# Three dense tiles of a graph-attention layer: turned matmuls, masked in place in SBUF

## The chip, the cores and the metric

The kernel runs on one core of one Trainium2 chip. The metric is the device time of one execution in microseconds (us). The time before is the median of three runs. One more execution was taken with the hardware profiler.

## The reference

Four graph-attention layers follow each other on 3327 nodes with 512 features. All use one sparse 0/1 adjacency matrix. Each layer normalizes its input, cuts it at zero, attends over the neighbours and adds the result to its input. The last layer, which the change touches, has eight heads of 64 features:

```python
Wh = jnp.einsum('ni,hio->hno', h, W)
f1 = jnp.einsum('hno,ho->hn', Wh, a1)
f2 = jnp.einsum('hno,ho->hn', Wh, a2)
e = jax.nn.leaky_relu(f1[:, :, None] + f2[:, None, :], ALPHA)
masked = jnp.where(adj[None] > 0, e, NEG_INF)
attention = jax.nn.softmax(masked, axis=-1)
h_prime = jnp.einsum('hnm,hmo->hno', attention, Wh)
```

The exponential of a leaky relu of a sum is a product of two exponentials, or a second product of two, whichever is larger. So the weight of a pair is, up to factors that cancel or go into the features, `max(a*b - 1, 0) + 1`. Here `a` belongs to the target node, `b` to the source node, and a factor `c` of the source is put on its features.

## The kernel before

**Tiles.** The nodes are padded to 3328, which is 26 tiles of 128 targets. They were ranked by degree before, so that tile 0 holds the nodes with most neighbours. `CAPS` says how many neighbours a tile's nodes may have: 36 for tile 0, 22 for tile 3, 11 for tile 25.

**List tiles.** In the last layer the tiles 25 down to 3 work from lists of neighbours. A step takes four columns of the list. `fetch` issues one indirect DMA (a gather, L835, on POOL) for each column but the first. Each brings 128 rows of 528 numbers from a table in DRAM into a buffer g. The first column is the node itself and comes by an ordinary DMA. There are five g buffers, and fetches run five steps ahead (`LOOK`). `scored` makes the weights: DVE adds (L888) and takes the leaky relu (L890), ACT takes the exponential into PSUM (pw, L891). `group` multiplies rows by weights on DVE (L919, 512 numbers a column, into a buffer m) and adds the columns up on PE with an identity as the stationary operand (L924, 512 columns into a PSUM bank). `divisors` and `means` (L942) divide, `added` (L958) adds the input, and `scatter` (L843) sends the tile out by an indirect DMA on POOL. All in all there are 360 gathers, 26 scatters and 105 steps.

**Dense tiles.** The tiles 0 to 2 (`DENSE[3] = 3`) attend to all 26 source blocks, with a mask of bytes for the adjacency. Class `Several` does this in two passes of four heads. The two passes over 26 blocks give 52 units `u`. For each unit:

- `load` brings the block's features (v, three buffers) and its mask (mk, three buffers), two DMAs on SP (L1259, L1260).
- `weights` makes four relus of 384 targets on ACT (L1276) into PSUM tile r, of which there is one.
- `features` scales the block's features by c on ACT (L1287) and puts c behind them (L1288), 65 numbers a head, into vs (two buffers).
- `masked` adds 1 and multiplies by the mask on DVE (L1292), one instruction over 1536 numbers, from r into e (two buffers in SBUF).
- `products` runs 12 matmuls on PE (L1310), one for each head and tile. The weights of 128 targets are stationary and the features of one head move. They are 65 columns, which `twice` doubles to 130. The results lie side by side in two PSUM banks, which a matmul with zeros (L1302) clears at the start of a pass.

At the end of a pass `means` (L1328, L1329) divides by the 65th column.

**The order.** PE, DVE, ACT and POOL execute their instructions in the order that is written. `later(s, place, piece)` hangs a piece of dense work on step `s`, ahead of `scored` ("first"), after it ("scored") or after `group` ("last"). `place` spreads the 52 units over the steps:

```python
for u in range(2 * NT):
    s = s0 + u * (s1 - s0) // (2 * NT)
    later(s, "first", lambda u=u: self.masked(u))
    later(s, "scored", lambda u=u: (self.weights(u + 1), self.features(u + 1), self.load(u + 3)))
    later(s + 1, "first", lambda u=u: self.products(u))
```

Here s0 is 0 and s1 is the number of steps less 8, so a unit comes about every 1.9 steps.

The other layers have no part in the change. Layer 1 uses `Several` for one tile of four heads, layer 2 has nine dense tiles of its own kind.

Of the kernel before, what the change touches and what calls it, by code (L numbers as in the profile page):

```python
# [18 lines left out]
P = 128  # L19
# [777 lines left out]
def tile_gat_lists(ctx: ExitStack, tc: tile.TileContext, x, adj, ws, avs, out, ident, half, slots, L, low, spare, tabx, tabs):  # L797
# [417 lines left out]
    class Several:  # L1215
# [3 lines left out]
        def __init__(self, l, n, W):  # L1219
            self.l, self.n, self.H, self.D = l, n, HEADS[l], F // HEADS[l]  # L1220
            self.Q = Q = self.H // 2
            self.DV = DV = self.D + 1
            self.tiles = [Tile(l, t, W) for t in range(n)]
            room = Room(low, L, spare, *([pools["e"].tile([P, 8 * BANK], F32, name="room", bufs=1)] if n > 1 else []))
            self.a = room(self.H * n * P).rearrange("p (h c) -> p h c", h=self.H)

            y = self.a.rearrange("p h c -> p (h c)")[:, -n * F:]
            self.y = [y[:, q * F:(q + 1) * F] for q in range(n)]
            self.e = [room(Q * n * P).rearrange("p (h c) -> p h c", h=Q) for _ in range(2)]
            self.c, self.b = [room(NT * Q * 2).rearrange("p (j h) -> p j h", j=NT) for _ in range(2)]  # L1230

            self.vs = [room((Q + (self.H == 8)) * DV) for _ in range(2)]
# [6 lines left out]
            self.per = BANK // DV - (self.H == 8)  # L1239

        def begin(self):

            if self.H == 8:
                for vs in self.vs:
                    nc.scalar.activation(vs[:, self.Q * self.DV:], ident[:, :self.DV], AF.Copy, scale=0.0)
# [49 lines left out]
        def products(self, u):  # L1295

            Q, DV = self.Q, self.DV
            j, e, vs = u % NT, self.e[u % 2], self.vs[u % 2]
            if j == 0:
                self.po = [pools["w"].tile([P, BANK], F32, name="whole") for _ in range(0, self.n * Q, self.per)]  # L1300
                for o in self.po:
                    nc.tensor.matmul(o, ident, zero.to_broadcast([P, BANK]), start=True, stop=False,  # L1302
                                     skip_group_check=True)
            for q in range(self.n):
                for h in range(Q):
                    o, o0 = self.where(q, h)
                    dst, mov = o[:, o0:o0 + DV], vs[:, h * DV:(h + 1) * DV]
                    if self.H == 8:
                        dst, mov = twice(dst, self.per * DV - o0), twice(mov, (Q - h) * DV)
                    nc.tensor.matmul(dst, e[:, h, q * P:(q + 1) * P], mov, start=False, stop=(j == NT - 1),  # L1310
                                     skip_group_check=True)

        def where(self, q, h):
            i = q * self.Q + h
# [18 lines left out]
        def place(self, s0, s1):  # L1333
# [12 lines left out]
            for q in range(self.n):  # L1346
                self.tiles[q].ends(s + 1 + 2 * q)

    at = {}

    def later(s, place, piece):
        at.setdefault((s, place), []).append(piece)
# [8 lines left out]
    for l in range(NL):  # L1361
        W, following = following, None
        if l == NL - 1:
            before.close()
        with ExitStack() as c2:
            def pool(name, bufs, **kw):
                return c2.enter_context(tc.tile_pool(name=f"{name}{l}", bufs=bufs, **kw))

            turning, projecting = [], []
            psum = dict(space=bass.MemoryType.PSUM)  # L1370
            whole = HEADS[l] == 1
            pools = {"o": pool("ps_o", 1 if whole else 2, **psum)}
            if l < NL - 1:
                pools.update(t=pool("ps_t", 1, **psum))
            if whole:
                pools.update(w=pool("ps_w", 3, **psum), e=pool("epool", 1))
                wholes = Wholes(l, W)
                pw = L[:, :BANK]
            else:
                pools.update(m=pool("mpool", 5))  # L1380
                pools.update(p=pool("ps_p", 1 if DENSE[l] else 2, **psum))
                if DENSE[l]:
                    pools.update(w=pool("ps_w", l // 3 + 1, **psum), r=pool("ps_r", 1, **psum))
                    if DENSE[l] > 1:
                        pools.update(e=pool("epool", 1))
                    wholes = Several(l, DENSE[l], W)
                    pw = pools["p"].tile([P, BANK], F32, name="pw")
            if not whole:

                for _ in range(2):  # L1390
                    nc.tensor.matmul(pools["o"].tile([P, BANK], F32, name="bank"), ident,
                                     zero.to_broadcast([P, BANK]), start=True, stop=True)
            if DENSE[l]:

                scores = itertools.cycle([pw[:, :BANK // 2], pw[:, BANK // 2:]])
            else:
# [84 lines left out]
```

## Time and profile before

| | |
|---|---|
| median of 3 runs | 2442.68 us (2439.82 to 2448.11) |
| profiled execution | 2959.5 us, span 2957.8 us |
| mean granted clock of PE | 0.867 |
| first gather of the last layer | 2296 us |
| PE, DVE, ACT, POOL busy in the last layer (662 us) | 524, 410, 204, 367 us |
| L924, 512 columns | 720 instructions in the layer's program, 0.43 us from start to start |
| L1310, 130 columns | 1248 instructions, 24 in 2.68 us |
| L1292, 1536 numbers | 52 instructions, 1.75 us each |
| L1276, 384 numbers | 208 instructions, 0.58 us each |
| L835, a gather | 0.95 us busy, 1.25 us from start to start |

The profiled execution is 517 us longer than the median, so its stretches are not stretches of a plain run. In the profile a matmul of 32-bit numbers is two instructions, each with a weight load of its own (PEld). A group's line shows its count, busy time, the mean of one, and the idle time of its engine just before, with what ended it. "issue" is waiting for which the profile shows nothing; "remote" is a wait whose end it can't put down to an instruction. A busy share says little here: POOL's next gather starts 0.30 us after the last one's busy time ends.

### The profile page before, as it was taken

Reading aid. Unit: us, or ns where it says so; the run is one execution under the profiler, and the core shown is the slowest. Engines: PE = TensorE matmul, PEld = TensorE weight load, DVE = VectorE, ACT = ScalarE, POOL = GpSimd, SP = SyncE. Lnnn points to the kernel's source line nnn. Section 1 sums busy time; section 2 is a strip of 40 time slices with the busy share of each in tenths; the row PEclk is TensorE's granted clock in tenths of the full one; section 3 lists DMA queues with packets and bytes.
Section 4 is the critical chain, followed back from the end, with each engine's and each line's share of the span. In section 5 each row is a group of like instructions: output and inputs, shape, how many; then the busy total and the mean of one; then the engine's idle time right before and its main releaser. Section 6 shows DMA issues by size and latency. Waiting matters only on the chain.

```text
span 2957.8 us, 27080 instructions
## 1 busy us (share of the span) xinstructions
PE 2224.7 (75%) x7082; PEld 1251.4 (42%) x7082; DVE 1914.3 (65%) x4968; ACT 931.8 (32%) x2502; POOL 1728.5 (58%) x1717
## 2 busy tenths in 40 slices
PE   4777677787677745788877787689696778877887
PEld 2664243343333323344434344245354445444453
DVE  7887656565546523767765565698887556666665
ACT  5882122222221101323332222344333333333330
POOL 7894465565556663555655552676764555555554
PEclk9988788888888877899988889799897889988898
DMA  6885477677666675666766663788775666666664
GB/s 229 322 294 160 140 218 216 193 235 222 188 205 195 189 194 170 181 202 192 209 193 189 192 192 111 226 264 257 236 248 152 191 177 184 185 182 194 185 187 137
DMA packets 260730, 594.20 MB, mean 201 GB/s; under 512 B 103699, under 2 KB 121107, under 8 KB 256214
## 3 DMA queue, kind: packets, MB, share of 16 engines
q0 software_dynamic: 124368, 432.13, 49.8%
q1 hardware_dynamic: 132454, 153.45, 16.5%
q10 hardware_dynamic: 3744, 6.82, 0.7%
q8 instruction: 57, 0.93, 0.1%
q14 instruction: 107, 0.88, 0.1%
HBM read 542.60 MB, written 49.65 MB: 200 GB/s over the span
## 4 chain that ended last, share of the span: by engine, by line
DVE 21%; PE 18%; issue 16%; another core or an unknown queue 11%; ACT 6%; POOL 4%; DMA 3%; DVEq 0%; ACTq 0%; POOLq 0%; SPq 0%
PE bank L924 11%; DVE m L919 9%; POOL g L835 3%; PE pv L469 3%; PE whole L1310 3%; DVE bank L912 2%; DMA g<-tab,idxb 1%; DVE z L890 1%; DVE z L888 1%; ACT r L1276 1%; DVE x L962 1%; DVE q L439 1%; ACT pw L891 1%; DVE room L1292 1%
## 5 line engine op out<-in xcount | busy, mean ns | idle before, releaser
L924 PE MATMUL bank<-m,ident 128*128 128x512 f32 x2414 | 1236.5, 659 | 268.9 <-DVE m L919 137.5
L835 POOL DMA_INDIRECT g<-tab,idxb x712 | 678.2, 952 | 465.5 <-issue 189.3
L919 DVE TENSOR_TENSOR m<-g,pw 128x512 f32<-128x512 f32 x1207 | 752.0, 682 | 267.6 <-ACT pw L891 193.5
L924 PEld LDWEIGHTS bank<-m,ident 128*128 128x128 f32 x2414 | 490.2, 211 | 879.8 <-issue 568.9
L469 PE MATMUL pv<-w,hT 128*128 128x264 f32 x1664 | 447.4, 423 | 107.0 <-ACT hT L458 71.2
L835 POOL DMA_INDIRECT g<-tabx,twiceb x342 | 324.1, 948 | 245.8 <-issue 124.4
L835 POOL DMA_INDIRECT g<-tab,idxa x297 | 283.1, 953 | 262.1 <-DMA tab<-v 88.5
L469 PEld LDWEIGHTS pv<-w,hT 128*128 128x128 f32 x1664 | 339.5, 208 | 215.2 <-ACT hT L458 79.6
L891 ACT ACTIVATE pw<-z 128x32 f32<-128x32 f32 (+4 forms) x356 | 67.8, 190 | 945.4 <-DVE z L890 509.8
L1162 PE MATMUL whole<-ve,em 128*128 128x512 f32 x468 | 224.5, 632 | 48.2 <-DVE em L1135 27.9
L1310 PE MATMUL whole<-L,room 128*128 128x130 f32 x1248 | 171.1, 288 | 79.2 <-issue 79.0
L1310 PEld LDWEIGHTS whole<-L,room 128*128 128x128 f32 x1248 | 163.1, 201 | 107.1 <-issue 104.7
L695 POOL TENSOR_TENSOR key<-a,keys 128x3328 int32<-128x3328 int32 (+1 forms) x29 | 189.5, 6539 | 15.9 <-DVE cand L704 12.6
L912 DVE SCALAR_TENSOR_TENSOR bank<-g,L,bank 128x512 f32<-128x512 f32 x243 | 183.3, 754 | 9.9 <-remote 2.0
L835 POOL DMA_INDIRECT g<-tabx,twicea x99 | 94.4, 954 | 119.6 <-issue 75.3
L1162 PEld LDWEIGHTS whole<-ve,em 128*128 128x128 f32 x468 | 92.8, 203 | 158.7 <-issue 114.6
L451 PE MATMUL pt<-ident,xn 128*128 128x128 f32 x416 | 74.5, 302 | 93.0 <-issue 32.2
L704 DVE MAX8 cand<-key 128x8 f32<-128x208 int32 x416 | 143.6, 363 | 0.1
L890 DVE SCALAR_TENSOR_TENSOR z<-z 128x32 f32<-128x32 f32 (+5 forms) x428 | 82.5, 193 | 91.4 <-remote 61.4
L919 DVE TENSOR_TENSOR bank<-g,pw 128x512 f32<-128x512 f32 x74 | 51.5, 696 | 126.7 <-ACT pw L891 105.6
L1276 ACT ACTIVATE r<-low,L 128x384 f32<-128x384 f32 x208 | 121.2, 582 | 9.8 <-remote 3.9
L888 DVE TENSOR_TENSOR z<-g,pw 128x32 f32<-128x32 f32 (+4 forms) x356 | 61.8, 174 | 94.9 <-DMA g<-tab,idxa 39.0
(181 smaller groups left out, 2154.4 us busy)
## 6 DMA issues: line engine op xcount, KB each, us to landing
a<-in_adj SPq DMA_DIRECT2D x25, 1664.0 KB
tab<-v SPq DMA_DIRECT2D x78, 264.0 KB
ve<-tab SPq DMA_DIRECT2D x78, 264.0 KB
g<-tab SPq DMA_DIRECT2D x65, 264.0 KB
tabx<-vx SPq DMA_DIRECT2D x26, 528.0 KB
g<-tab,idxb POOLq DMA_INDIRECT x712
low<-tab SPq DMA_DIRECT2D x52, 132.0 KB
spare<-tab SPq DMA_DIRECT2D x52, 132.0 KB
```

Of the source, the lines that this page charges most:

```text
L469: nc.tensor.matmul(pv[:, s, :HF + 8], hT[:, k, :], W.w[:, k, s, :], start=(k == 0), stop=(k == KC - 1))
L695: nc.gpsimd.tensor_tensor(key[:, c:c + quarter], a[:, c:c + quarter], keys[:, c:c + quarter], OP.mult)
L704: nc.vector.max(cand[:, g * 8:(g + 1) * 8], key[:, g * SEG:(g + 1) * SEG])
L835: nc.gpsimd.indirect_dma_start(out=out_, out_offset=None, in_=table, in_offset=bass.IndirectOffsetOnAxis(ap=which, axis=0))
L890: nc.vector.scalar_tensor_tensor(z, z, SLOPE, z, OP.mult, OP.max)
L891: nc.scalar.activation(self.wt[:, k0:k0 + n, :H], z, AF.Exp)
L912: nc.vector.scalar_tensor_tensor(acc, v, w, acc, OP.mult, OP.add)
L919: nc.vector.tensor_tensor(out_.rearrange("p (s h d) -> p s h d", s=2, d=D), v.rearrange("p s (h d) -> p s h d", d=D), wt[:, k0 + q, :H].re ...
L924: nc.tensor.matmul(self.po, ident, m[:, q, :], start=False, stop=(k0 + q == K - 1), skip_group_check=True)
L1162: nc.tensor.matmul(tl.po.rearrange("p (s m) -> p s m", s=2), e[:, q * P:(q + 1) * P], v.rearrange("p (s m) -> p s m", s=2)[:, :, :F // 2], ...
L1276: nc.scalar.activation(self.r[:, h, :], self.a[:, g, :], AF.Relu, bias=-1.0, scale=self.b[:, j, g:g + 1])
L1310: nc.tensor.matmul(dst, e[:, h, q * P:(q + 1) * P], mov, start=False, stop=(j == NT - 1), skip_group_check=True)
```

## The change

The last layer's dense tiles get a class of their own, `Turned`; `Several` is left to layer 1 and loses what only eight heads needed. In `Turned` the operands of the matmul change places. The scaled features of one head (65 columns) are stationary, and the weights of all three tiles (384 columns) move. So a unit has 4 matmuls in place of 12, and the results of a head (65 x 384) take one PSUM bank, four banks for a pass. The relus are written to the SBUF buffer e, and the mask is applied there in place. The buffers e, vs, v and mk are rings of four. At the end of a pass ACT copies the sums to SBUF, PE turns them back, 65 x 128 at a time, and DVE divides. The units are spread in half steps, and there are four steps between the passes.

```diff
+    class Turned:
+        def __init__(self, l, n, W):
+            self.l, self.n, self.H, self.Q, self.D = l, n, HEADS[l], 4, F // HEADS[l]
+            self.DV = self.D + 1
+            self.passes = self.H // self.Q
...
+            self.e = [room(self.Q * wide).rearrange("p (h c) -> p h c", h=self.Q) for _ in range(4)]
+            self.sums = self.a[:, self.Q:, :]
...
+            self.vs = [room(self.Q * self.DV) for _ in range(4)]
+            self.v = [room(self.Q * self.D + 8) for _ in range(4)]
+            self.mk = [room(n * P // 4).bitcast(U8) for _ in range(4)]
...
+        def weights(self, u):
...
+            e = self.e[u % 4]
+            for h in range(Q):
+                nc.scalar.activation(e[:, h, :], self.a[:, h0 + h, :], AF.Relu, bias=-1.0,
+                                     scale=self.b[:, j, h0 + h:h0 + h + 1])
+
+        def features(self, u):
...
+            vs = self.vs[u % 4].rearrange("p (h d) -> p h d", d=self.DV)
+            for h in range(Q):
+                nc.scalar.activation(vs[:, h, :D], self.v[u % 4][:, h * D:(h + 1) * D], AF.Copy,
+                                     scale=self.c[:, j, h0 + h:h0 + h + 1])
+            nc.scalar.activation(vs[:, :, D], self.c[:, j, h0:h0 + Q], AF.Copy)
+
+        def masked(self, u):
+            n = self.n * P
+            nc.vector.scalar_tensor_tensor(self.e[u % 4], self.e[u % 4], 1.0,
+                                           self.mk[u % 4].unsqueeze(1).to_broadcast([P, self.Q, n]), OP.add, OP.mult)
+
+        def products(self, u):
+            j, e, vs, DV = u % NT, self.e[u % 4], self.vs[u % 4], self.DV
+            if j == 0:
+                self.po = [pools["w"].tile([P, BANK], F32, name="whole") for _ in range(self.Q)]
+            for h, o in enumerate(self.po):
+                nc.tensor.matmul(o[:DV, :self.n * P], vs[:, h * DV:(h + 1) * DV], e[:, h, :], start=(j == 0),
+                                 stop=(j == NT - 1))
+
+        def summed(self):
+            for h, o in enumerate(self.po):
+                nc.scalar.activation(self.sums[:self.DV, h, :], o[:self.DV, :self.n * P], AF.Copy)
+
+        def turned(self, q):
+            DV = self.DV
+            self.pt = pools["x"].tile([P, BANK], F32, name="turned")[:, :self.Q * DV].rearrange("p (h d) -> p h d", d=DV)
+            for h in range(self.Q):
+                nc.tensor.transpose(self.pt[:, h, :], self.sums[:DV, h, q * P:(q + 1) * P], ident[:DV, :DV])
...
+        def place(self, s0, s1):
+            later(s0 - 1, "first", self.begin)
+            for u in range(4):
+                later(s0 - 1, "first", lambda u=u: self.load(u))
+            later(s0 - 1, "scored", lambda: (self.weights(0), self.features(0)))
+            halves = 2 * (s1 - s0 - 4 * (self.passes - 1))
+            for u in range(self.passes * NT):
+                i, j = divmod(u, NT)
+                s, b = divmod(2 * (s0 + 4 * i) + u * halves // (self.passes * NT), 2)
+                place = "last" if b else "first"
+                later(s, place, lambda u=u: self.masked(u))
+                later(s, "last" if b else "scored",
+                      lambda u=u: (self.weights(u + 1), self.features(u + 1), self.load(u + 4)))
+                later(s + 1, place, lambda u=u: self.products(u))
+                if j == NT - 1:
+                    later(s + 3, "scored", self.summed)
+                    for q in range(self.n):
+                        later(s + 4 + 2 * q, "first", lambda q=q: self.turned(q))
+                        later(s + 5 + 2 * q, "last", lambda i=i, q=q: self.means(i, q))
+            for q in range(self.n):
+                self.tiles[q].ends(s + 5 + 2 * q)
...
-                    pools.update(w=pool("ps_w", l // 3 + 1, **psum), r=pool("ps_r", 1, **psum))
-                    if DENSE[l] > 1:
-                        pools.update(e=pool("epool", 1))
-                    wholes = Several(l, DENSE[l], W)
+                    many = DENSE[l] > 1
+                    pools.update(w=pool("ps_w", 4 if many else 1, **psum))
+                    if many:
+                        pools.update(e=pool("epool", 1), x=pool("ps_x", 1, **psum))
+                    else:
+                        pools.update(r=pool("ps_r", 1, **psum))
+                    wholes = (Turned if many else Several)(l, DENSE[l], W)
...
-                wholes.place(0, len(steps) - 8)
+                wholes.place(0, len(steps) - (12 if many else 8))
```

In the changed program the relu is L1404, the features L1414, the mask L1420, the matmul L1429, the copy of the sums L1434, the turn L1440 and the means L1445 and L1449. Lines up to 1231 keep their numbers.

More of the change, by code (lines that the diff above doesn't have):

```diff
@@ L1230, in __init__ @@
             self.c, self.b = [room(NT * Q * 2).rearrange("p (j h) -> p j h", j=NT) for _ in range(2)]
-            self.vs = [room((Q + (self.H == 8)) * DV) for _ in range(2)]
+            self.vs = [room(Q * DV) for _ in range(2)]
             self.v = [room(ROW // 2) for _ in range(3)]
@@ L1238, in __init__ @@
                                   tabs[l % 2][t * P:(t + 1) * P, F // 2:F // 2 + self.H])
-            self.per = BANK // DV - (self.H == 8)
+            self.per = BANK // DV
         def begin(self):
-            if self.H == 8:
-                for vs in self.vs:
-                    nc.scalar.activation(vs[:, self.Q * self.DV:], ident[:, :self.DV], AF.Copy, scale=0.0)
             for q in range(self.n):
@@ L1306, in products @@
                     o, o0 = self.where(q, h)
[L1307 to L1311, printed above, removed]
+                    nc.tensor.matmul(o[:, o0:o0 + DV], e[:, h, q * P:(q + 1) * P], vs[:, h * DV:(h + 1) * DV],
+                                     start=False, stop=(j == NT - 1), skip_group_check=True)
         def where(self, q, h):
@@ L1347, in place, with begin, first_head, load @@
                 self.tiles[q].ends(s + 1 + 2 * q)
+    class Turned:
[3 more added lines that the diff above has]
+            self.passes = self.H // self.Q
+            self.tiles = [Tile(l, t, W) for t in range(n)]
+            room = Room(low, L, spare, pools["e"].tile([P, 17 * BANK], F32, name="room", bufs=1))
+            wide = n * P
+            self.a = room(self.H * wide).rearrange("p (h c) -> p h c", h=self.H)
+            y = room(n * F)
+            self.y = [y[:, q * F:(q + 1) * F] for q in range(n)]
+            self.e = [room(self.Q * wide).rearrange("p (h c) -> p h c", h=self.Q) for _ in range(4)]
+            self.sums = self.a[:, self.Q:, :]
+            self.c, self.b = [room(NT * self.H).rearrange("p (j h) -> p j h", j=NT) for _ in range(2)]
+            self.vs = [room(self.Q * self.DV) for _ in range(4)]
+            self.v = [room(self.Q * self.D + 8) for _ in range(4)]
+            self.mk = [room(n * P // 4).bitcast(U8) for _ in range(4)]
+            self.s = room(n * 8).rearrange("p (t h) -> p t h", h=8)
+            for t in range(n):
+                nc.sync.dma_start(self.s[:, t, :self.H],
+                                  tabs[l % 2][t * P:(t + 1) * P, F // 2:F // 2 + self.H])
+        def begin(self):
+            for q in range(self.n):
+                for h0 in range(0, self.H, 4):
+                    pa = pools["x"].tile([P, BANK], F32, name="turned").rearrange("p (h c) -> p h c", c=P)
+                    for h in range(4):
+                        nc.tensor.matmul(pa[:, h, :], self.s[:, q, h0 + h:h0 + h + 1].to_broadcast([P, P]), ident,
+                                         start=True, stop=True)
+                    nc.scalar.activation(self.a[:, h0:h0 + 4, q * P:(q + 1) * P], pa, AF.Exp, scale=1.0 - SLOPE)
+        def first_head(self, i):
+            return self.H - (i + 1) * self.Q
+        def load(self, u):
+            if u < self.passes * NT:
+                i, j = divmod(u, NT)
+                h0 = self.first_head(i)
+                c0 = h0 * self.D + (8 if 2 * h0 >= self.H else 0)
+                n = self.Q * self.D + (8 if i == 0 else 0)
+                nc.sync.dma_start(self.v[u % 4][:, :n], tabs[self.l % 2][j * P:(j + 1) * P, c0:c0 + n])
+                nc.sync.dma_start(self.mk[u % 4].bitcast(I32), masks[0, j, :, :self.n * P // 4])
+        def weights(self, u):
+            if u == self.passes * NT:
+                return
+            i, j = divmod(u, NT)
+            Q, H = self.Q, self.H
+            h0 = self.first_head(i)
+            if i == 0:
+                d = self.v[u % 4][:, Q * self.D:Q * self.D + H]
+                nc.scalar.activation(self.b[:, j, :], d, AF.Exp, scale=1.0 - SLOPE)
+                nc.scalar.activation(self.c[:, j, :], d, AF.Exp, scale=SLOPE)
+            e = self.e[u % 4]
[3 more added lines that the diff above has]
+        def features(self, u):
+            if u == self.passes * NT:
+                return
+            i, j = divmod(u, NT)
+            Q, D, h0 = self.Q, self.D, self.first_head(i)
+            vs = self.vs[u % 4].rearrange("p (h d) -> p h d", d=self.DV)
[22 more added lines that the diff above has]
+                nc.tensor.transpose(self.pt[:, h, :], self.sums[:DV, h, q * P:(q + 1) * P], ident[:DV, :DV])
+        def means(self, i, q):
+            Q, D, h0 = self.Q, self.D, self.first_head(i)
+            den = small.tile([P, Q], F32, name="den3")
+            nc.vector.reciprocal(den, self.pt[:, :, D])
+            tl = self.tiles[q]
+            tl.y = self.y[q]
+            y = tl.y[:, h0 * D:(h0 + Q) * D].rearrange("p (h d) -> p h d", d=D)
+            nc.vector.tensor_tensor(y, self.pt[:, :, :D], den.unsqueeze(2).to_broadcast([P, Q, D]), OP.mult)
+        def place(self, s0, s1):
[5 more added lines that the diff above has]
+            for u in range(self.passes * NT):
+                i, j = divmod(u, NT)
+                s, b = divmod(2 * (s0 + 4 * i) + u * halves // (self.passes * NT), 2)
[9 more added lines that the diff above has]
+                        later(s + 5 + 2 * q, "last", lambda i=i, q=q: self.means(i, q))
+            for q in range(self.n):
+                self.tiles[q].ends(s + 5 + 2 * q)
```

## The prediction

> **What bounds the kernel now.** I read the engine totals first, then the stretch of the last layer by windows, then that stretch's waits and timeline. The change touches only the last layer. Its first gather starts at 2296 us of the profile, and the span ends at 2958.
>
> ```profile
> span 2957.8 us, 27080 instructions
> PE 2224.7 (75%) x7082; PEld 1251.4 (42%) x7082; DVE 1914.3 (65%) x4968; ACT 931.8 (32%) x2502; POOL 1728.5 (58%) x1717
> ```
>
> The window row of this layer (length, then busy time and instructions of PE, PEld, DVE, ACT, POOL, granted clock, DMA share, GB/s):
>
> ```profile
> 2296.00:2958.00 662.00, 523.96 (x2020) 310.54 (x2018) 409.62 (x801) 203.85 (x631) 366.52 (x386) 0.89 0.63 181
> ```
>
> PE looks fullest (524 of 662 us). But a POOL gather costs more than its busy time. The groups of POOL in the same window:
>
> ```profile
> L835 POOL DMA_INDIRECT g<-tab,idxb x261 | 247.1, 947 | 199.6 <-issue 70.8 <-DVE m L919 52.5 <-DVE z L888 38.2
> L835 POOL DMA_INDIRECT g<-tab,idxa x99 | 93.7, 947 | 81.8 <-issue 29.9 <-DVE m L919 21.5 <-DMA tab<-v 10.1
> ```
>
> The timeline shows back-to-back gathers 1.25 us apart: 0.95 busy and 0.30 of issue that waits for nothing shown. 360 gathers at 1.25 us and 26 scatters (L843) at 1.29 us are 480 us of demand; the other 182 us POOL waits, mostly for DVE to free a gather buffer. By the same count, POOL after 274 us (first gather) has 1963 us of demand and 721 us of waiting. The median run is 2442.7 us, 517 us less than the profiled execution (2959.5 us; the span is 1.7 us shorter). If work costs the same in both, only 2443 - 274 - 1963 = 206 us of that waiting is left unprofiled, 29%. For this layer that is 52 us, so the layer takes about 532 us unprofiled. Some 37 us of the 52 are its ends: 26 us before the gathers run (waits of 16.4 and 10.1 us at 2286 and 2296) and 10.6 us before the last scatter. So POOL is nearly full there, if its 0.30 us is no product of profiling.
>
> What stretches the profiled layer are the waits:
>
> ```profile
> ACT L L1287 <- remote: 109.1, 25, 10.1
> DVE m L919 <- ACT pw L891: 85.5, 44, 10.9
> PE whole L1310 <- issue: 79.0, 58, 2.6
> POOL g L835 <- DVE m L919: 74.0, 16, 7.9
> ```
>
> They form one loop. PE stops inside a burst of L1310 for nothing shown, as here:
>
> ```profile
> 2707.76 2.84 PE L1310 MATMUL whole<-L,room 128*128 128x130 f32 x24
> ...
> 2717.31 2.06 PE L1310 MATMUL whole<-L,room 128*128 128x130 f32 x17
> 2720.52 0.27 PE L1310 MATMUL whole<-L,room 128*128 128x130 f32 x1 [1.15 <-issue]
> 2723.36 0.27 PE L1310 MATMUL whole<-L,room 128*128 128x130 f32 x1 [2.57 <-issue]
> ```
>
> ACT's features (L1287) then wait for PE to let go of one of two vs buffers (the waits put down to "remote" end with a count of PE's own semaphore), the next exponentials (L891) stand behind them, DVE's products (L919) wait for those, and POOL waits for DVE.
>
> **The rule of the skill.** The Trainium skill, page "SBUF — State Buffer", section "SBUF: two separate sides", says that DVE and GpSimd share one port pair, which a DVE instruction with two SBUF inputs holds for its whole length against a GpSimd instruction that reads SBUF. The trace of before agrees. L956 has both inputs in SBUF for some tiles and one in PSUM for others:
>
> ```profile
> 1782.25 0.69 DVE L956 SCALAR_TENSOR_TENSOR low<-ex,low 128x512 f32<-128x512 f32 x1
> 1782.35 1.40 POOL L835 DMA_INDIRECT g<-tab,idxb  x1 [0.30 <-issue]
> ```
>
> The gather started inside the DVE instruction and took 1.40 us against a median of 0.946: it was stretched to that instruction's end plus 0.82 us. I looked at all gathers and scatters over 1.0 us in the trace: 28, of which 26 began while a DVE instruction with two SBUF inputs ran (L956, L962, L408); the others are the very first gather and a scatter of 1.01, where 0.99 is usual. Today's mask reads r in PSUM, and a gather inside it is untouched:
>
> ```profile
> 2668.86 1.72 DVE L1292 SCALAR_TENSOR_TENSOR room<-r,spare 128x1536 f32<-128x1536 f32 x1
> ...
> 2669.75 0.95 POOL L835 DMA_INDIRECT g<-tab,idxb  x1 [0.30 <-issue]
> ```
>
> After the change, L1420 reads e and the mask, both in SBUF. The forecast goes by the rule and by these rows together.
>
> **The change part by part.** A unit is one source block in one pass; there are 52.
>
> PE, removed: per unit 24 instructions of 130 columns (12 matmuls, each two instructions), 2.68 us in the chain of waits. Added: 4 matmuls, so 8 instructions of 384 columns. A 512-column L924 goes at 6.87 us for 16, so 0.839 ns a column; 8 x 384 x 0.839 = 2.58 us. The gain is 52 x 0.10 = 5 us. The eight zeroing instructions (L1302, 0.43 us each) go, 3.4 us. Twenty-four turns of 65 columns come; no such shape is in the trace, L451's 128-column turn (302 ns with latency) bounds one, so 0 to 7 us; I take 2. Sum: -6 us, and the shape's own cost could be off by 10% of 134 us, so -19 to +8.
>
> PE, stops: 79 us lie inside these bursts. With 416 matmul instructions for 1248, their share would fall by two thirds, -53 us profiled. Unprofiled they may not exist: the profile is 517 us longer, and stops that nothing explains make up 16% of its chain (some 470 us). From 0 to -53 us, I take 0 for the median.
>
> DVE, the mask: 52 instructions of 1536 elements before and after. 1.75 us each stays (L956 is 0.689 from two SBUF inputs and 0.690 with one in PSUM). Means: 12 small instructions for 16, nothing.
>
> POOL, the lock: a gather that starts in the first 1.63 us of a 1.75 us mask is held to its end (1.75 less the 0.12 us which the 0.82 above leaves). Gathers start every 1.25 us, so each mask catches one, and the delay is 0.38 to 1.63 us, mean 1.0. 52 x 1.0 = 52 us on POOL's stream: 480 becomes 532. If the mask falls where POOL has just been released by DVE, 1.6 each, 83 us; if POOL waits anyway, nothing. Behind a held gather stand all later gathers; DVE's z (L888) is late next, then L919 and PE.
>
> ACT: 208 relus of 384, now into SBUF; 582 ns before. L948 takes 615 ns from SBUF and 583 from PSUM, so a change of memory is worth about 30 ns; 208 x 30 = 6 us on an engine busy 204 of 662. Eight copies of the sums (some 0.6 us) add 5 us. Both hide beside POOL's stream; without that cover, 11 us. The wait of L1287 on PE goes: a ring of four gives each buffer two more units, about 20 us. This frees at most POOL's remaining waiting, 52 - 37 = 15 us unprofiled.
>
> DMA and SP: 104 loads before and after, 48 to 132 KB, 256 columns for 264 in half of them; issued four units ahead for three. POOL issues the same instructions in the same order. Nothing: no wait above is on a load, and if one came late ACT's relus would be late next, with three units of some 10 us each (532 / 52) in hand. The dense work is packed into 12 steps fewer than the layer has (8 before), and its tiles end at step 100 for 101 of 105: nothing.
>
> **The sum.** For the profiled execution: +52 of lock, less what POOL's 182 us of waiting absorbs, -53 of PE stops, and less ACT wait: 2959.5 falls to about 2920. For the median: +52 (lock) - 15 (POOL waiting that ends) - 6 (PE, hidden, so 0) = +37 if POOL is full throughout; if it is not, the same lock falls on waiting time and gives 0 to +37. I take the middle, +19: 2442.7 + 19 = 2462 us.
>
> **The rivals.** (1) Slower by the lock, as above: 2450 to 2500, the upper end with 1.6 us a mask. For it: the 26 of 28 rows and POOL's sum. Against: the sum assumes that 1.25 us holds unprofiled. (2) Faster: PE with its stops is the bound also unprofiled, and POOL keeps waiting time that swallows the lock. It decides if over some 40 us of L1310's stops are real, or if POOL's 0.30 us of issue is an effect of profiling; then 360 x 0.3 = 108 us more waiting is there to swallow the 52. Price: -6 of columns and up to -53 of stops, middle -30: 2413, from 2385 to 2435. For it: L1287's 109 us and the 79. Against: POOL's account of the whole run fits in the median with little left. (3) Nothing measurable: lock and relief cancel, 2443. (4) The change doesn't do what it says: if the four buffers did not free ACT, only the lock remains, +52, 2495. The order of instructions shows 208 matmuls of 65x384 for 624 in the program, so the reshaping itself happens.
>
> **The numbers.** Under 0.3%, 7.3 us, can't be told from no change. Slower (1 and 4) 0.50, faster 0.36, same 0.14. The point is case 1's 2462. The range of 8 in 10 takes in most of case 2: 2402 to 2500; case 1's own is 2450 to 2500.
>
> **What would show it.** L835 beside L1420: gathers of 1.3 to 2.5 us where they began inside it, near 52 of them, and a mean above 1.0 us in this layer. L1429 at 0.32 us start to start with few stops inside its bursts. L1404 and L1414 no longer waiting for PE; L919 waiting less for L891. POOL's waiting in the layer under 100 us profiled. The prediction is wrong if gathers inside L1420 stay at 0.95 us, or if they stretch and the median still falls: then POOL was not the bound.

## The result and the profile after

| | before | after |
|---|---|---|
| median of 4 runs each | 2441.25 us (2438.57 to 2448.11) | 2484.50 us (2483.31 to 2489.83) |
| ratio | | 1.0178, 95% interval 1.0163 to 1.0193 |

The change costs 43.3 us. The forecast was 19 us, so the direction was right and the size less than half.

One thing has to be known before the two profiles are compared. The profile of before that the prediction reads shows PE stopping inside its bursts, and on one chip the kernel before showed the same again and took 2920 us in plain runs (first experiment below). The runs of both medians and the profile of after come from chips on which PE does not stop. I therefore show after beside a later profile of the kernel before on a chip without the stops (called before*; 2446.6 us, span 2444.8).

The head of the page of after:

```profile
span 2488.1 us, 25486 instructions
PE 2072.9 (83%) x6266; PEld 1102.9 (44%) x6266; DVE 1920.7 (77%) x4964; ACT 922.1 (37%) x2508; POOL 1781.7 (72%) x1717
```

The profiled run took 2489.83 us, 0.2 to 0.3% more than the other three (2483.31 to 2485.49). So here the profile stands for the timed runs.

The last layer by windows, first before*, then after (length, then busy time and count of PE, PEld, DVE, ACT, POOL; clock, DMA share, GB/s):

```profile
1936.00:2445.00 509.00, 471.91 (x2018) 283.67 (x2017) 409.78 (x801) 200.86 (x631) 366.68 (x386) 0.97 0.78 235
```

```profile
1936.00:2489.00 553.00, 475.04 (x1200) 199.48 (x1200) 412.79 (x797) 194.50 (x639) 419.02 (x386) 0.97 0.75 216
```

PE, DVE and ACT hardly move. POOL's busy time grows by 52.3 us over the same 386 instructions. The layer grows by 44. The groups of POOL say where, again before* first (these two answers start at 1850 us, so 37 of the 298 gathers belong to the layer before):

```profile
L835 POOL DMA_INDIRECT g<-tab,idxb x298 | 283.2, 950 | 92.0 <-issue 70.2 <-DVE m L919 7.9 <-DMA g<-tab,idxb 7.0
...
L835 POOL DMA_INDIRECT g<-tab,idxa x99 | 93.8, 947 | 47.3 <-issue 23.8 <-DMA tab<-v 10.2 <-DVE den L930 6.0
```

```profile
L835 POOL DMA_INDIRECT g<-tab,idxb x298 | 317.7, 1066 | 89.9 <-issue 75.7 <-DVE m L919 5.5 <-DMA g<-tab,idxb 4.6
...
L835 POOL DMA_INDIRECT g<-tab,idxa x99 | 109.5, 1106 | 40.0 <-issue 25.0 <-DMA tab<-v 10.2 <-DMA g<-tab,idxa 2.1
```

The mean of a gather goes from 0.950 and 0.947 us to 1.066 and 1.106. Of the layer's own 261 gathers in the first line it goes from 0.947 to 1.080. Counted as the gaps between POOL's instructions less the usual 0.30 us, POOL waits 20.4 us in the layer of after, 9.9 before the first gather and 10.5 before the last scatter, so nothing lies between. In before* it waits 29.3 us, 9.9 and 10.0 at these two places and 9.4 between. One line of the waits shows it, before* first (in us, times, longest; a wait of 0.3 us is the usual gap):

```profile
POOL g L835 <- DVE m L919: 10.9, 30, 2.1
```

```profile
POOL g L835 <- DVE m L919: 6.4, 21, 0.3
```

The timeline of after shows one held gather:

```profile
1989.51 1.75 DVE L1420 SCALAR_TENSOR_TENSOR room<-room 128x1536 f32<-128x1536 f32 x1
1989.58 2.50 POOL L835 DMA_INDIRECT g<-tab,idxa  x1 [0.30 <-issue]
...
1992.39 0.95 POOL L835 DMA_INDIRECT g<-tab,idxa  x1 [0.30 <-issue]
```

The mask ends at 1991.26 and the gather 0.82 us later, as the prediction read it off L956. The next one follows at the usual 0.30 us, so the delay is passed on whole. Each of the 52 masks holds exactly one instruction of POOL's stream: 49 gathers and 3 scatters, which are counted as gathers from here on. The excess over the usual length (0.946 us, a scatter 0.988) is 52.7 us in sum, 1.01 us in the mean.

The rest of the change did what it says. In the groups of after, the relus and the matmuls stand with no idle time before them:

```profile
L1404 ACT ACTIVATE room<-low,L 128x384 f32<-128x384 f32 x208 | 110.5, 601 | 0.0
...
L1429 PE MATMUL whole<-room,L 128*65 128x384 f32 x312 | 107.0, 486 | 0.0
L1420 DVE SCALAR_TENSOR_TENSOR room<-room 128x1536 f32<-128x1536 f32 x39 | 68.1, 1746 | 0.0
```

The waits of the layer show DVE now waiting for gathers to land, where before* has 12.5 and 17.3 us (the first two lines) and 42.7 us (the third):

```profile
DVE z L888 <- DMA g<-tab,idxb: 62.0, 32, 4.3
DVE z L888 <- DMA g<-tab,idxa: 32.1, 11, 17.5
DVE m L919 <- ACT pw L891: 25.5, 79, 0.6
```

### The profile page after: what moved, and what is told of

Read it like the earlier page. It is cut to its first block, busy times and chain, and to the rows that moved or that the text cites. A ratio compares the mean times of both kernels' runs of the same rounds, so it can differ in the third digit from the quotient of the medians.

```text
span 2488.1 us, 25486 instructions
## 1 busy us (share of the span) xinstructions
PE 2072.9 (83%) x6266; PEld 1102.9 (44%) x6266; DVE 1920.7 (77%) x4964; ACT 922.1 (37%) x2508; POOL 1781.7 (72%) x1717
## 4 chain that ended last, share of the span: by engine, by line
DVE 29%; DMA 23%; POOL 15%; issue 12%; PE 12%; ACT 7%; DVEq 0%; SPq 0%; ACTq 0%; POOLq 0%
POOL g L835 12%; DVE m L919 12%; DMA g<-tab,idxb 9%; PE pv L469 5%; DMA g<-tabx,twiceb 5%; DMA g<-tab,idxa 5%; PE bank L924 3%; DVE bank L912 2%; DVE z L890 2%; DVE z L888 2%; ACT pw L891 1%; DMA g<-tabx,twicea 1%; PE pi L786 1%; POOL key L695 1%; DMA vx<-in_x 1%
## 5 line engine op out<-in xcount | busy, mean ns | idle before, releaser
L924 PE MATMUL bank<-m,ident 128*128 128x512 f32 x2414 | 1142.0, 618 | 178.7 <-DVE m L919 177.7
L835 POOL DMA_INDIRECT g<-tab,idxb x712 | 712.4, 1001 | 243.0 <-issue 170.5
L924 PEld LDWEIGHTS bank<-m,ident 128*128 128x128 f32 x2414 | 453.8, 196 | 749.5 <-DVE m L919 374.9
L469 PE MATMUL pv<-w,hT 128*128 128x264 f32 x1664 | 439.5, 419 | 65.9 <-ACT hT L458 43.7
L891 ACT ACTIVATE pw<-z 128x32 f32<-128x32 f32 (+4 forms) x356 | 68.8, 193 | 1046.3 <-DVE z L890 1046.1
L469 PEld LDWEIGHTS pv<-w,hT 128*128 128x128 f32 x1664 | 337.3, 206 | 167.4 <-ACT hT L458 49.5
L835 POOL DMA_INDIRECT g<-tab,idxa x297 | 298.6, 1005 | 156.4 <-issue 70.6
L1404 ACT ACTIVATE room<-low,L 128x384 f32<-128x384 f32 x208 | 110.5, 601 | 0.0
L1128 ACT ACTIVATE r<-low,mc,b 128x384 f32<-128x384 f32 x78 | 52.6, 675 | 147.2 <-DVE em L1135 124.5
L1429 PE MATMUL whole<-room,L 128*65 128x384 f32 x312 | 107.0, 486 | 0.0
L451 PE MATMUL pt<-ident,xn 128*128 128x128 f32 x416 | 65.4, 281 | 47.1 <-ACT hT L458 18.3
L890 DVE SCALAR_TENSOR_TENSOR z<-z 128x32 f32<-128x32 f32 (+5 forms) x428 | 80.8, 189 | 14.7
L451 PEld LDWEIGHTS pt<-ident,xn 128*128 128x128 f32 x416 | 52.5, 145 | 81.0 <-issue 33.3
```

The costliest lines, as they stand in the source:

```text
L451: nc.tensor.transpose(pt[:, k, :], xn[:, k * P:(k + 1) * P], ident)
L469: nc.tensor.matmul(pv[:, s, :HF + 8], hT[:, k, :], W.w[:, k, s, :], start=(k == 0), stop=(k == KC - 1))
L835: nc.gpsimd.indirect_dma_start(out=out_, out_offset=None, in_=table, in_offset=bass.IndirectOffsetOnAxis(ap=which, axis=0))
L890: nc.vector.scalar_tensor_tensor(z, z, SLOPE, z, OP.mult, OP.max)
L924: nc.tensor.matmul(self.po, ident, m[:, q, :], start=False, stop=(k0 + q == K - 1), skip_group_check=True)
L1404: nc.scalar.activation(e[:, h, :], self.a[:, h0 + h, :], AF.Relu, bias=-1.0, scale=self.b[:, j, h0 + h:h0 + h + 1])
```

## Experiments on a chip where TensorE stops

The theory: a mask with both inputs in SBUF holds one gather of POOL's stream each time, and since POOL is full, this is the whole loss. The rival: something else in the new order (half steps, the ring, the turned sums) costs the 43 us. The first four runs, with the kernel before beside them, happened to run on a chip of the kind that the first profile shows.

**before_again.** The kernel before, unchanged.

> The kernel before, profiled a second time. If the stops of PE in the first profile (79 us inside L1310, and others in layers that the change does not touch) belong to that one execution, they are gone here: a span near 2440 us, POOL waiting under 20 us between its first gather and its last in the last layer, no gather inside L1292 over 1.0 us. If they belong to the kernel or to profiling it, the span is again near 2950 us.

Eleven other runs of the kernel before on this chip had a median of 2919.63 us (2911.53 to 2929.99); the profiled one took 2932.77. So the extra time is no effect of that one profiled execution, and the 517 us that the prediction put down to profiling belong to the chip. (Which chip the first profile came from is not on record; its stops, and its granted clock of 0.867 against 0.872 here and 0.938 in before*, are of this kind.) The last layer takes 645.9 us from its first gather, POOL waits 166 us of them, and the waits of PE show the same stops as the first profile:

```profile
PE whole L1310 <- issue: 57.8, 47, 3.2
```

Before* has no such line among its waits; there L1310 has 0.0 us of idle time before it.

**lock_only.** The kernel before, with the relus' tile r in SBUF instead of PSUM, so that only the place of one tile differs, which ACT writes and the mask (here L1296) reads. (The SBUF room of the class grows from 8 to 12 banks' length for it.)

```diff
+            self.rs = room(Q * n * P).rearrange("p (h c) -> p h c", h=Q) if n > 1 else None
...
-            r = pools["r"].tile([P, self.n, BANK], F32, name="r").rearrange("p a b -> p (a b)")
-            self.r = r[:, :Q * n].rearrange("p (h c) -> p h c", h=Q)
+            if self.rs is not None:
+                self.r = self.rs
```

> The kernel before with one thing changed: the relus write r to SBUF in place of PSUM, so that the mask has two SBUF inputs; matmuls, buffers and order stay. If the hold on POOL is the cost: 52 gathers stretched, 52 us in sum, time 2441 + 52 less at most 10 us of waiting that POOL had, 2483 to 2493. If the cost of the change lies in the turned matmuls, the sums or the rings: no change, 2441 within 7 us.

2895.79 us, ratio 0.9914 (0.9890 to 0.9938). Of the gathers that began inside a mask, 50 were held, by 49.9 us in sum; in before_again 72 began inside one and none was held. The layer did not get longer, since POOL's waiting in it fell from 166 to 103 us. That the time fell by 24 us is not explained: in the profiles, 29 us of difference lie ahead of the layer, in code that the edit doesn't touch.

**mask_in_psum.** The changed kernel, with the mask copied by ACT into one place in PSUM for each unit (L1405), so that the mask instruction (L1423) reads e in SBUF and the mask in PSUM. The turned sums move to free columns of pw's bank.

```diff
+            nc.scalar.activation(self.pm, self.mk[u % 4], AF.Copy)
...
-                                           self.mk[u % 4].unsqueeze(1).to_broadcast([P, self.Q, n]), OP.add, OP.mult)
+                                           self.pm.unsqueeze(1).to_broadcast([P, self.Q, n]), OP.add, OP.mult)
```

> The changed kernel with ACT copying each unit's mask into PSUM (52 more copies of 384, some 0.6 us each), so that the mask instruction has one input in SBUF and one in PSUM; the sums are turned two heads at a time to find room. If the hold on POOL is the cost: no gather stretched by the mask, and the time of the changed kernel less its 52.7 us of stretching, 2432 (2425 to 2441). If the cost lies elsewhere in the change: 2484 or a little more for the copies.

2897.02 us, ratio 0.9911 (0.9888 to 0.9935). No gather was held.

**mask_by_head.** The changed kernel with the mask in four instructions of 384 numbers a unit (L1421).

```diff
-            nc.vector.scalar_tensor_tensor(self.e[u % 4], self.e[u % 4], 1.0,
-                                           self.mk[u % 4].unsqueeze(1).to_broadcast([P, self.Q, n]), OP.add, OP.mult)
+            for h in range(self.Q):
+                nc.vector.scalar_tensor_tensor(self.e[u % 4][:, h, :], self.e[u % 4][:, h, :], 1.0,
+                                               self.mk[u % 4], OP.add, OP.mult)
```

> The changed kernel with the mask applied head by head, 208 instructions of 384 in place of 52 of 1536, still two SBUF inputs. DVE pays 208 x 0.61 = 127 us for 91. If the hold on POOL is the cost, a gather is held only when it starts in the first 0.49 us of an instruction: 0.39 of them, 0.25 us each, 0.10 us x 208 = 20 us in place of 52.7: 2452 (2445 to 2462). If DVE's own time were the cost: 36 us slower than the changed kernel, 2520; if the cost lies elsewhere, 2484.

2874.22 us, ratio 0.9853 (0.9816 to 0.9890); 68 gathers held, 12.8 us in sum.

On this chip the kernel with the whole lock takes less time than before, and so does one without any. Here POOL isn't full, and the lock's price can't be read from the total. The premise of the prediction's second rival (PE with its stops is the bound) fits this chip. Whether the changed kernel gains there is open, since it was not run there.

## The same kernels on a chip where TensorE doesn't stop

The same kernels were run again beside the changed one, and beside the kernel before, which took 2439.32 us (19 runs).

**after_b**, the changed kernel:

> The changed kernel itself, on the chip of this set of runs. There are chips on which PE stops for nothing shown and the kernel before takes 2920 us, and chips on which it takes 2441. Where PE does not stop: 2484, all 52 gathers that begin inside the mask stretched. Where PE stops: PE sets the pace there, POOL has over 100 us of waiting in the last layer that takes the stretching in, and a third of the matmul instructions meets fewer stops, so the changed kernel is faster than the kernel before, 2860 to 2900 against 2920.

**lock_only_b:**

> The kernel before with the relus written to SBUF alone, so that the mask has two SBUF inputs. Where PE does not stop: if the hold on POOL is the cost, 2441 + 52 less at most 10, 2483 to 2493; if the turned matmuls, sums or rings are the cost, 2441. Where PE stops: 2896 as in the first set.

**mask_by_head_b:**

> The changed kernel with the mask in 208 instructions of one head, still two SBUF inputs. The first set showed them at 0.55 us and 68 gathers held, 12.8 us in sum, with POOL waiting in between. Where PE does not stop: if the hold on POOL is the cost, a hold of 0.43 us at most, 0.34 of the instructions, 0.21 us each, 15 us in sum, 2447 (2440 to 2456); if DVE's own time were the cost, slower than the changed kernel by 208 x 0.55 - 91 = 23 us, 2507. Where PE stops: 2874.

**mask_in_psum_b:**

> The changed kernel with each unit's mask copied into PSUM by ACT, so that the mask instruction has one SBUF input. Where PE does not stop: if the hold on POOL is the cost, 2484 less 52.7, 2432 (2425 to 2441); if it lies elsewhere, 2484 or a little more. Where PE stops: 2897 as in the first set.

after_b took 2483.20 us, ratio 1.0181 (1.0157 to 1.0205), 52 gathers held by 51.2 us. lock_only_b took 2482.77, ratio 1.0176 (1.0159 to 1.0193), 52 held by 53.9 us. So moving one tile of the old kernel to SBUF reproduces the loss of the whole change. Its gathers, by groups:

```profile
L835 POOL DMA_INDIRECT g<-tab,idxb x294 | 316.6, 1077 | 88.8 <-issue 70.8 <-DMA g<-tab,idxb 7.3 <-DVE m L919 7.0
```

mask_by_head_b took 2446.85, ratio 1.0033 (1.0025 to 1.0040), with 69 gathers held by 12.8 us. It writes the same numbers to the same buffers in the same order as the changed kernel, only in shorter instructions. DVE has more to do than in the changed kernel (208 x 0.55 = 115 us for 91), and the kernel is still 36 us faster, so DVE's own time is not the cost. A gather held by a 0.55 us instruction loses little:

```profile
L835 POOL DMA_INDIRECT g<-tab,idxb x295 | 288.5, 978 | 89.1 <-issue 67.2 <-DVE m L919 7.9 <-DMA g<-tab,idxb 7.3
...
L1421 DVE SCALAR_TENSOR_TENSOR room<-room 128x384 f32<-128x384 f32 x156 | 76.3, 552 | 0.0
```

mask_in_psum_b was a miss: 2507.86 us, ratio 1.0281 (1.0264 to 1.0298). No gather was held, yet POOL waited 94.6 us in the layer. The waits point to a cause in the edit itself:

```profile
DVE m L919 <- ACT pw L891: 93.9, 80, 3.5
...
ACT turned L1405 <- DVE room L1423: 54.4, 14, 4.6
ACT turned L1405 <- issue: 49.5, 12, 4.3
...
POOL g L835 <- DVE z L888: 34.2, 18, 6.2
```

There is one place for the mask in PSUM, so ACT's copy for the next unit waits for DVE's mask of this one. The exponentials (L891) stand behind it on ACT, DVE's products wait for those, and POOL for DVE. For the 49.5 us under issue the profile shows no cause.

## Half the lock, none of it, and the kernel before again

Two more kernels vary the dose, and the third run gives the profile called before* above; the kernel before took 2442.22 us beside them (11 runs).

**mask_two.** As mask_in_psum, with the copies going to two places in turn, the second one in the free columns of three banks of the products.

```diff
+            self.w = pools["w"].tile([P, self.Q, BANK], F32, name="whole")
+            self.pm = [self.xb[:, :n * P], self.w[:, :n, n * P:]]
```

> The masks of two successive units are copied by ScalarE into two places in PSUM in turn (the second split over three banks, so its unit takes three VectorE instructions of 512 elements in place of one of 1536), so ScalarE's copy for unit u+1 no longer waits for the mask of unit u. Lock theory with the single buffer as the reason for the miss of the run with one copy: no gather stretched in the last layer, GpSimd idle there by 35 us or less beyond its 0.30 us between gathers, and on a chip on which TensorE does not stop 2425 to 2450 us against 2440 of the kernel before. Rival (the one-copy kernel lost its time because ScalarE has 19 us more to do or because VectorE reads PSUM, not because of the single copy): 2490 to 2510. On a chip on which TensorE stops: 2850 to 2890 under the first, no less than 2895 under the rival.

A second miss: 2533.30 us, ratio 1.0372 (1.0356 to 1.0389). No gather was held, and POOL waited 118 us. The second place brought a new wait. It shares banks with the products' sums, and the copy and the mask wait for PE:

```profile
DVE room L1427 <- PE whole L1436: 53.2, 19, 6.3
...
ACT whole L1407 <- PE whole L1436: 51.4, 20, 4.8
```

So the changed kernel without any lock and without another wait was not measured, and these two runs don't exclude the rival that ACT's 52 copies or DVE's reading of the mask from PSUM cost the time. That the lock is the cause rests on lock_only_b and on the doses.

**mask_half.** As mask_in_psum, with the copy and its use only in every second unit; the others keep both inputs in SBUF.

```diff
+            if u % 2 == 0:
+                nc.scalar.activation(self.pm, self.mk[u % 4], AF.Copy)
...
+                                           (self.mk[u % 4] if u % 2 else self.pm).unsqueeze(1)
+                                           .to_broadcast([P, self.Q, n]), OP.add, OP.mult)
```

> Half the dose: the mask of every second unit is read from PSUM (one copy, which now has a whole unit more before it is needed again), the other 26 keep both operands in SBUF. Lock theory: 26 gathers stretched by 1.0 us each, 26 us in sum, and halfway between the changed kernel and the one with two copies: 2450 to 2465 us where TensorE doesn't stop (2483 less 26 is 2457). If the cost did not come by the instruction but by having the mask in SBUF at all, or from other parts of the change: 2475 to 2490. Where TensorE stops: 2865 to 2895 under lock theory.

2458.97 us, ratio 1.0074 (1.0059 to 1.0090), as the theory has it, with 26 copies by ACT and 26 masks read from PSUM. 26 gathers were held, by 24.1 us in sum. The two kinds of unit stand in one timeline, with the same instruction of nearly the same length:

```profile
2101.04 1.70 DVE L1424 SCALAR_TENSOR_TENSOR room<-room,turned 128x1536 f32<-128x1536 f32 x1
2101.20 0.95 POOL L835 DMA_INDIRECT g<-tab,idxb  x1 [0.30 <-issue]
```

```profile
2127.64 1.79 DVE L1424 SCALAR_TENSOR_TENSOR room<-room 128x1536 f32<-128x1536 f32 x1
2127.65 0.95 POOL L835 DMA_INDIRECT g<-tab,idxb  x1 [0.30 <-issue]
...
2128.90 1.36 POOL L835 DMA_INDIRECT g<-tab,idxb  x1 [0.30 <-issue]
```

With the mask in PSUM (turned) the gather inside keeps 0.95 us. With it in SBUF, the gather that began 0.01 us after the mask isn't held, and the next one is, to 0.83 us after the mask's end (2127.64 + 1.79, against 2128.90 + 1.36).

**before_c** (before*).

> The kernel before, for a profile on the chip of these runs. If TensorE does not stop on it: the last layer from the first gather to the end takes 505 to 512 us, of which GpSimd is idle 10 to 30 us beyond its 0.30 us between gathers, so that it is as full there as in the changed kernel and every microsecond of lock counts. If instead GpSimd is idle by 50 us or more there, as the prediction took it, the lock should have been absorbed in part and the full cost of the change needs another reason. On a chip on which TensorE stops: 640 to 650 us and 160 us idle, as in the earlier repeat.

508.7 us from the first gather to the end, and POOL waits 29.3 us: 9.9 at the start, 10.0 before the last scatter, 9.4 between.

With that the doses can be set side by side. The third column takes off the 9.4 us of waiting that the kernel before has between its gathers. The fourth is the time from the layer's first gather to the end, in the profile of each, less the 508.7 us of before*:

| kernel | gathers held, sum | less 9.4 us | layer in the profile | median against before |
|---|---|---|---|---|
| mask_by_head_b | 69, 12.8 us | 3.4 | +2.8 us | +7.5 us |
| mask_half | 26, 24.1 us | 14.7 | +18.2 us | +16.8 us |
| after_b | 52, 51.2 us | 41.8 | +40.5 us | +43.9 us |
| after (first result) | 52, 52.7 us | 43.3 | +43.9 us | +43.3 us |
| lock_only_b | 52, 53.9 us | 44.5 | +46.5 us | +43.5 us |

The lock's sum and one constant, which was measured and not fitted, give all five times within about 4 us.

## A version meant to beat both

**four_tiles.** Since POOL's stream sets the layer, a fourth tile is taken from the lists, with the mask half from PSUM and half by head. The ring has three buffers so that it fits.

```diff
-DENSE = [0, 1, 9, 3]
+DENSE = [0, 1, 9, 4]
...
+            if u % 2 == 0:
+                nc.vector.scalar_tensor_tensor(self.e[u % 3], self.e[u % 3], 1.0,
+                                               self.pm.unsqueeze(1).to_broadcast([P, self.Q, n]), OP.add, OP.mult)
+            else:
+                for h in range(self.Q):
+                    nc.vector.scalar_tensor_tensor(self.e[u % 3][:, h, :], self.e[u % 3][:, h, :], 1.0,
+                                                   self.mk[u % 4], OP.add, OP.mult)
```

> A version meant to beat both kernels: what the runs showed is that the last layer is as long as GpSimd's chain of gathers, so the work is taken from that chain. Four tiles are dense instead of three (the fourth has 22 gathers, 22 x 1.25 = 27.5 us of GpSimd less), the moving weights are 512 columns, the ring has three buffers, and the lock is kept small: every second unit reads its mask from PSUM, the others take four instructions by head. Lock left, by the run with the mask by head: 104 short instructions, half as many but 0.73 us long instead of 0.55, about 8 to 12 us. Sum against the kernel before where TensorE does not stop: 2442 - 27 + 10 = 2425 us, range 2415 to 2440. Rival: TensorE, whose dense products grow by a third (208 products, some 0.1 us each, 21 us), becomes the bound before GpSimd gives the 17 us: 2440 to 2460. Where TensorE stops: 2840 to 2890.

2478.60 us against 2442.47, ratio 1.0144 (1.0118 to 1.0171): no gain, and over both ranges. The lock was as small as expected (26 held, 8.1 us), but POOL now waits 72 us. In one stretch of the layer PE is busy all of the 150 us:

```profile
2250.00:2400.00 150.00, 150.00 (x350) 58.38 (x349) 130.75 (x248) 70.91 (x197) 108.73 (x112) 1.00 0.78 231
```

There PE may well be the bound. It isn't shown for the layer, where PE is busy 489 of 539 us, no larger a share than in before* (472 of 509). The turned sums, which go through pw's bank in this version, add waits that the expectation had left out:

```profile
DVE z L888 <- PE pw L1450: 30.3, 13, 6.4
POOL g L835 <- DVE den L1455: 26.5, 11, 8.8
```

The ring, the PSUM copy, the turns and the fourth tile were changed together here, so PE's share in the loss isn't separated from theirs. No version of these beats the kernel before.

## Why the prediction was right in kind and wrong in size

- **The rule and the lock's size: right.** The Trainium skill, page "SBUF — State Buffer", section "SBUF: two separate sides", and the two L956 rows gave one held gather a mask, to the mask's end plus 0.82 us, 52 x 1.0 = 52 us. Measured: 52 of 52 held, 52.7 us, 1.01 us each. The control, an operand in PSUM, left 0 of 66 gathers held in before*.
- **The step that failed: "if it is not, the same lock falls on waiting time and gives 0 to +37. I take the middle, +19".** That case did not occur. POOL was full in the runs that count: between its gathers it waits 9.4 us in before* and nothing in after. So the sum for a full POOL, +37 or 2480 us, stood, and halving it moved the point to 2462, 22 us under what came. The doubt came from the stops in the profile, which the text itself called possibly absent from a plain run.
- **The term of 15 us: too large, and near by luck.** "POOL waiting that ends" was 9.4 us, because before* has only that much between its gathers. With it the sum is 52.7 - 9.4 = 43.3, and 43.3 were measured. The working of the 15 has two errors that partly cancel. The 52 us of waiting, 29% of the 182 us counted from 2296 us on, were too many: before* waits 29.3 us. The 37 us of ends that were taken off hold 16.4 us at 2286 us, ahead of that count. By the text's own rows the ends are 10.1 and 10.6 us, so the term would have been 31 us and the sum +21.
- **The 517 us: wrong cause, useful count.** They were called a difference between the profile and a plain run. By before_again they are a difference between chips. The demand of POOL, 480 us for the layer, held on both kinds, since it counts POOL's own durations; before* has 508.7 less 29.3 = 479.4. So did the 0.30 us of issue: it is there in the profile of after, which is within 0.3% of the other runs.
- **ACT's wait of about 20 us: too large here.** L1287 waits 7.2 us for PE in before*, and POOL's 9.4 us of waiting between its gathers bound what a deeper ring can bring. The 109 us of the first profile are of the chip with stops.
- **PE: hidden as said.** L1429 starts every 0.32 us, as forecast. PE's busy time changed from 472 to 475 us in the layer, and it isn't what the layer waits for.
- **Rivals.** The second (faster) was decided by whether PE's stops are real in the runs that count. They are real on one chip, and the runs that count don't have them. The fourth (only the lock remains) gives +52, or 2495, 11 us over what came. Of that difference 9.4 is explained: the 9.4 us of waiting did go.

## What to carry to other kernels

Before a tensor-tensor operation on DVE is moved from PSUM to SBUF, count what POOL issues meanwhile. If gathers run back to back, each long instruction with two SBUF inputs delays the stream by up to its own length (1.55 us at most for a mask of 1.75 us in after), and only waiting that the stream has anyway makes up for it. Keep one operand in PSUM, as the kernel before does, or cut the instruction to less than the gather's pitch: here four pieces of 0.55 us cost 13 us of holding where one of 1.75 us cost 51. Copying an operand into PSUM for every instruction removed the hold and brought other waits that cost more (2507.86 and 2533.30 us).

When a profiled execution is a fifth longer than the median, its waits may not be those of the timed runs. Build the sum from the durations of the engine that is nearly full, and if that says full, take the full sum, not half of it.

## What the runs showed of the hardware

Chips differ in a way that can hide what a change costs. The kernel before takes 2920 us on one and 2440 us on others, with the same instructions. On the slower one PE stops inside bursts for nothing the trace shows, 57.8 us in L1310 alone. The kernel with the whole lock and no other change takes 0.9% less time than before there and 1.8% more on the other; that the gain comes from the edit isn't shown.

What makes PE stop wasn't found. The granted clock is lower where it stops, 0.872 in before_again against 0.938 in before*. But in the first profile only 113 of the 245 us of PE's stops over 0.7 us that stand under issue fall where the clock was granted at half, so the clock alone doesn't account for them.

The hold acts on the start of a gather. In after, 42 gathers were under way when a mask began, and none of them took more than 0.99 us. In mask_half one that began 0.01 us after the mask was not held, while the next, 1.26 us into it, was. In mask_by_head_b 5 of the 74 gathers that began inside a short mask were not stretched: one began 0.005 us after the mask's start, and four in its last 0.12 us, where a gather of the usual length ends as late as a held one.
